# One tile of adj held for tests in layer 1, and table switches kept out from a logarithm's table load to its use

## The chip, the cores and the metric

One core of one Trainium2 chip. The metric is the device time of one execution in microseconds. The core has five engines with a queue each: TensorE (PE in the profile, its weight loads PEld), VectorE (DVE), ScalarE (ACT), GpSimd (POOL) and SyncE (SP), which here only issues transfers. Each queue runs in the order in which the program was written out; engines wait for each other through semaphores.

## The reference

Four graph layers over the same 4096 x 4096 matrix adj of zeros and ones (0.8% ones) and features x of 4096 x 64. Each layer adds its result to x after a layer norm and a relu.

```python
h = relu(layernorm(x)); x = x + L0(h, adj)   # weights 2^-(place among the last 100 neighbours), by a running count
h = relu(layernorm(x)); x = x + L1(h, adj)   # att = adj * sigmoid(scores(q, k)); support = att @ h; scaled
h = relu(layernorm(x)); x = x + L2(h, adj)   # twice: m = adj @ (x @ W); GRU gates with sigmoid and tanh
h = relu(layernorm(x)); x = x + L3(h, adj)   # hyperbolic: norms, artanh (logarithms), tanh, adj @ (gamma * X)
```

Layer 3's lines that matter here:

```python
_artanh(x) = arctanh(clip(x, -ARTANH_BOUND, ARTANH_BOUND))
mobius_matvec: res = tanh(mx_norm / x_norm * artanh(x_norm)) * (mx / mx_norm)
```

## The kernel before

The kernel keeps all of adj, transposed, in on-chip memory as 8-bit numbers (tiles A). Its 4096 columns are cut into four quarters q of 1024, worked on one after another; within a quarter the 4096 rows are 32 blocks of 128. The fast path is valid only where adj holds nothing but zeros and ones, so a second reading of adj in full precision is tested beside the other work: tiles named whole, 128 x 1024, 512 KB each, one DVE instruction and an accumulator read per tile. The count of other values goes through a small PE matmul (flag_ps) into a flag, which selects a general path at the end. There are 128 such tests in all. The generator checks() (lines 1102 to 1126) issues each transfer on SP's queue and then the test on DVE; the variable depth says how many further tiles it may have loaded beyond the test that is next. It was set to 2 in layer 0 (lines 1218 and 1221) and stays so in layer 1; in layer 2 it is 4.

Layer 1 (stream1, line 1347) takes a quarter in sixteen double blocks, two at a time. For each double block and each half c of the columns, score() makes two PSUM banks of scores on PE, weigh() (line 1328) takes the sigmoid of both on ACT into one tile sig and multiplies it with adj on DVE, and add() multiplies it with S on PE into the quarter's accumulators acc. So a pair of double blocks is 16 short score matmul records, 16 acc records, four sig tiles. The tiles sig and the tiles whole come from one pool, b4p (line 812), with six buffers:

```python
    b4p = ctx.enter_context(tc.tile_pool(name="fb4", bufs=6))
                loaded.append(b4p.tile([P, 2 * CW], F32, tag="b4", name="whole"))
        g = b4p.tile([P, 2, CW], F32, tag="b4", name="sig")
```

A new tile gets a buffer that an earlier one leaves, and its first writer (a transfer or a sigmoid) waits for the earlier tile's last reader. When a quarter ends, its accumulators are copied (mt) and added (agg), and post1 runs a long row of small steps beside the next quarter: the transpose ps_n, norms, a layer norm, the split into bf16 parts (hm, rest, lo) and the transpose ps_t.

The order of all this is written out beforehand by a planner, the class Weave. It books a guessed time for each instruction. The main loops issue their instructions directly; side work (generators such as post1, pre3, post3, checks) hands out one operation (Op) at a time, and draw() and fill() place it where begin(op) plus its guessed length fits before a limit. For DVE and ACT that limit is PE's planned time plus 0.4 plus weave.late, which is 1.0 in layer 1 once layer 0's side work is over (line 1375). Nothing of the planner runs on the chip; it fixes the order only.

Layer 3 prepares its features in pre3 (line 1638), once for each quarter, beside layer 2's second step and layer 3's first sums: two squares (of h and of mxn), their sums, lengths() (an inverse square root of twelve small DVE steps), artanh2() with two logarithms on ACT, a tanh, then three bf16 parts written to S3. ACT needs another table for the logarithm than for sigmoid or tanh. preload() runs a dummy activation (void) so that the table load stands early. Meanwhile the gates of layer 2's last quarter also use ACT: sigmoids r and z, and a tanh on r; then three DVE steps on xT and the transpose ps_o. Layer 3's sums (sum3) fill PSUM banks acc3, two for each of eight output blocks u; a new bank waits until its former reader is through. post3 does the last norm, artanh and tanh, and stores.

Of the kernel before, what the change touches and what calls it, by code (L numbers as in the profile page):

```python
# [12 lines left out]
AF = mybir.ActivationFunctionType  # L13
# [580 lines left out]
class Op:  # L594


    def __init__(self, e, dur, ins, outs, run, kinds=()):
        self.e, self.dur, self.ins, self.outs, self.run, self.kinds = e, dur, ins, outs, run, kinds


def names(*aps):
    return [a.tensor.name for a in aps if isinstance(a, bass.AP)]


class Weave:
# [10 lines left out]
    def __init__(self):  # L616
        self.t = dict.fromkeys("PDAGS", 0.0)
        self.at, self.used = {}, {}
        self.banks = {1: [0.0] * 8}
        self.kind = {}  # L620
        self.work, self.back, self.width = [], [], 2
        self.late = 0.0
        self.quiet = False
        self.dma = 0.0
        self.busy = False
        self.table = None
        self.tiled = 0

    def ready(self, e, ins, outs=(), kinds=()):
        s = 0.0  # L630
# [46 lines left out]
            (self.work if piece in self.work else self.back).remove(piece)  # L677

    def begin(self, op):
        return max(self.t[op.e], self.ready(op.e, op.ins, op.outs, op.kinds))  # L680

    def issue(self, piece):
# [62 lines left out]
TABLES = {AF.Sigmoid: 0, AF.Tanh: 0, AF.Ln: 1, AF.Exp: 2}  # L745


class Engine:
# [12 lines left out]
    def __getattr__(self, name):  # L761
        fn, w = getattr(self.real, name), self.weave

        def call(*args, **kw):
            outs = names(args[0], kw.get("accum_out"))
            ins = names(*args[1:], *(v for k, v in kw.items() if k != "accum_out"))
            n = max(math.prod(a.shape[1:]) for a in args if isinstance(a, bass.AP))
            dur = self.cost(name, n) if name != "dma_start" else 0.1
            if "accum_out" in kw:
                dur += 0.08  # L770

            def run():
                more = 0.0
                if name == "activation" and args[2] in TABLES:
                    more = 1.3 if w.table != TABLES[args[2]] else 0.0
                    w.table = TABLES[args[2]]
                w.book(self.e, dur + more, ins, outs)
                if name == "dma_start":
                    for k in outs:
                        w.land(k, 1.4 if "whole" in k else 0.8)  # L780
                return fn(*args, **kw)  # L781

            if self.later:
                return Op(self.e, dur, ins, outs, run)
            if self.e in "DA":
                w.fill(self.e, w.ready(self.e, ins, outs) + w.late)
            return run()
        return call
# [3 lines left out]
def fast_kernel(ctx: ExitStack, tc: tile.TileContext, t: dict, out: bass.AP, flag: bass.AP):  # L792
# [24 lines left out]
    weave = Weave()  # L817
# [282 lines left out]
    depth = [1]  # L1100
# [246 lines left out]
    def stream1():  # L1347

        acc, behind = [], []

        def add(c, q, i, gs):
            if i == 0:
                acc.append(one(f"acc{c}"))
            for j in range(2):
                b = 2 * i + j
                mm(acc[c][j * D:(j + 1) * D, :], S1[b // QB][:, b % QB, :], gs[c][:, j, :],
                   start=i == 0, stop=i == NB // 2 - 1)

        def add_behind(more=()):
            q, i, gs = behind.pop(0)  # L1360
            for c in (0, 1):
                add(c, q, i, gs)
                if more:
                    more.pop(0)()
                weave.draw(weave.quiet)
            if i == NB // 2 - 1:
                weave.finish()
                weave.add(post1(q, acc[:]))
                acc.clear()

        def turn(q, i, later=None):
            if q == 0 and i % (QB // 2) == 0:
                weave.until((1, i // (QB // 2)), DONE)
            weave.quiet = (1, NQ - 1) not in DONE
            weave.late = 2.0 if weave.quiet else 1.0
            gs = ahead[:] if (q, i) == (0, 0) else []
            for c in range(len(gs), 2):
                ps = score(q, i, c)
                if later is None:
                    gs.append(weigh(q, i, c, ps))  # L1380
                else:
                    later.append(lambda q=q, i=i, c=c, ps=ps: gs.append(weigh(q, i, c, ps)))
                weave.draw(weave.quiet or c == 1)
            behind.append((q, i, gs))
            if i == 8:
                load1(q + 1)

        for q in range(NQ):
            for i in range(0, NB // 2, 2):

                later = []
                turn(q, i)
                turn(q, i + 1, later)
                while len(behind) > 2:
                    add_behind(later)
                for go in later:
                    go()
                if len(behind) > 1:
                    add_behind()
        add_behind()  # L1400
# [193 lines left out]
        yield from pre3(q)  # L1594


    def lengths(s):

        yield DV.tensor_scalar(s, s, NORM_EPS2, None, op0=ALU.max)
        r = yield from rsqrt(s)  # L1600
        n = stat("norm", s.shape[1])
        yield DV.tensor_tensor(n, s, r, ALU.mult)
        return n, r
# [5 lines left out]
    def preload(func):  # L1609

        yield AC.activation(void, tab, func)

    def artanh2(x, between=()):

        nb = x.shape[1]
        xc = stat("axc", nb)
        yield DV.tensor_scalar(xc, x, ARTANH_BOUND, None, op0=ALU.min)
        q, r = stat("at", nb), stat("ln", nb)
        yield AC.activation(q, xc, AF.Ln, bias=ones)
        yield AC.activation(r, xc, AF.Ln, bias=ones, scale=-1.0)  # L1620
        yield from preload(AF.Tanh)
        low = small.tile([P, ST], I32, tag="st", name="flow")[:, :nb]
        yield DV.tensor_scalar(low, xc, 0.25, None, op0=ALU.is_lt)
        x2, p = stat("x2", nb), stat("po", nb)
        yield DV.tensor_tensor(x2, xc, xc, ALU.mult)
        yield DV.tensor_scalar(p, x2, *(2.0 * c for c in ARTANH_POLY[:2]), op0=ALU.mult, op1=ALU.add)
        yield DV.tensor_tensor(p, p, x2, ALU.mult)
        for c in ARTANH_POLY[2:-1]:
            yield DV.scalar_tensor_tensor(p, p, 2.0 * c, x2, op0=ALU.add, op1=ALU.mult)
        yield DV.tensor_tensor(q, q, r, ALU.subtract)  # L1630
        yield DV.scalar_tensor_tensor(p, p, 2.0 * ARTANH_POLY[-1], xc, op0=ALU.add, op1=ALU.mult)
        yield from between
        yield DV.copy_predicated(q, low, p)
        return q
# [3 lines left out]
    def pre3(q):  # L1638
# [8 lines left out]
        ss = stat("ss", 2 * QB)  # L1647
        for i, v in enumerate((hn, mx)):
            sq = b2("sq")
            yield AC.activation(sq, v, AF.Square)  # L1650
            yield DV.tensor_reduce(ss[:, i * QB:(i + 1) * QB], sq, AX.X, ALU.add)
        yield from preload(AF.Ln)
        n, r = yield from lengths(ss)
        mr, c = r[:, QB:], stat("ratio", QB)
        yield DV.tensor_tensor(c, n[:, QB:], r[:, :QB], ALU.mult)
        a = yield from artanh2(n[:, :QB])
# [10 lines left out]
        e = D + 1  # L1667
# [133 lines left out]
    def post3(parts3, sgn, den, ss):  # L1801

        nb = CB * len(parts3)
        part = [slice(i * CB, (i + 1) * CB) for i in range(len(parts3))]
        vs = [n65[:, :, :D] for u, (n65, al) in parts3]
        yield from head3(len(parts3) - 1, parts3[-1][1], sgn, den, ss)  # L1810
        yield from preload(AF.Ln)
        rd = yield from recip(den)
        n, r = yield from lengths(ss)
        t = stat("t", nb)
        yield DV.tensor_tensor(t, n[:, :nb], rd, ALU.mult)
        ratio = stat("ratio", nb)

        def between():
            yield DV.tensor_tensor(ratio, n[:, nb:], r[:, :nb], ALU.mult)

        a = yield from artanh2(t, between())
        for h, (u, (n65, al)) in zip(part, parts3):
            yield DV.scalar_tensor_tensor(a[:, h], a[:, h], 0.25, al, op0=ALU.mult, op1=ALU.mult)
        yield DV.scalar_tensor_tensor(a, a, ARTANH_MAX, ratio, op0=ALU.min, op1=ALU.mult)
        yield AC.activation(a, a, AF.Tanh)
        yield DV.tensor_tensor(a, a, r[:, nb:], ALU.mult)
        for h, v, (u, (n65, al)) in zip(part, vs, parts3):
            yield DV.scalar_tensor_tensor(v, v, 0.0, rows(a[:, h]), op0=ALU.max, op1=ALU.mult)
            x = X[u // 2][:, (u % 2) * CB:(u % 2 + 1) * CB, :]
            yield DV.tensor_tensor(x, x, v, ALU.add)  # L1830
            yield SY.dma_start(out_nm[:, u * CB:(u + 1) * CB, :], x)
# [8 lines left out]
    weave.add(pre0(NQ - 2))  # L1840
    stream0()
    lead[0] = math.inf
    stream1()
    depth[0] = 4
    for step in range(2):
# [89 lines left out]
```

## Time and profile before

| | us |
|---|---|
| median of 3 runs | 806.51 (806.50 to 806.54) |
| the profiled execution | 807.01 |
| its span in the profile | 805.1 |
| mean granted TensorE clock | 0.993 |

| stage | from, to in the span (us) |
|---|---|
| layer 0 (and the start of layer 1's side work) | 0 to about 240 |
| layer 1 | about 240 to 497 |
| layer 2, two steps | 497 to about 691 |
| layer 3's sums | in between, from about 691 to 790.6 |
| the last rows | 790.6 to 805.1 |

How to read it: a row of the timeline or the chain starts with the time from the span's start and a length. A group row names line, engine, operation, output<-input with shapes, and count; most DVE and ACT rows have line 781 and the PE rows 973, since helpers record them, so tiles are told apart by name. "[1.35 <-DVE whole]" means that the engine had been idle for 1.35 us and that this instruction of DVE, which writes or reads whole, released it. A run "x16" of PE is merged from 16 records, and its length can hold short pauses between them.

### The profile page before, as it was taken

The page shows a single profiled execution, that of the slowest core. Times are in us where ns is not written, and L with a number is a line of the kernel's source. Part 1 is how long each engine was busy: PE and PEld are TensorE (multiplying, and loading weights), DVE is VectorE, ACT ScalarE, POOL GpSimd, SP SyncE. Part 2 cuts the span into 40 slices and gives each one's busy share as a digit, 9 for nine tenths or more (in the row PEclk, how much of TensorE's full clock was granted, in tenths as well). Part 3 has the DMA queues.
Part 4 walks back from the last instruction along what each step waited for, and adds up shares of the span by engine and source line. Part 5 has one row for each costly group of instructions (what it writes and reads, how often), then busy time and mean ns, then how long its engine had stood idle before and what let it go on. Part 6 is the DMA issues. An engine that isn't in the chain of part 4 may idle for free.

```text
span 805.1 us, 12309 instructions
## 1 busy us (share of the span) xinstructions
PE 767.5 (95%) x4473; PEld 369.7 (46%) x4494; DVE 635.6 (79%) x1419; ACT 432.2 (54%) x756; POOL 61.6 (8%) x125
## 2 busy tenths in 40 slices
PE   5999999999999999998999999999999999999992
PEld 2334444544443333332333333444444444599992
DVE  6886867777777988988888898978789387685895
ACT  5655555565566777887787785113220245444333
POOL 3333233231000000000000000000000000000000
PEclk9999999999999999999999999999999999999997
DMA  9999999999601033013104006696888300000010
GB/s 220 153 174 193 217 163 207 205 177 207 183 34 40 0 118 93 25 59 99 52 25 130 30 1 210 225 361 215 287 304 313 76 8 20 1 2 2 9 35 17
DMA packets 43956, 98.41 MB, mean 122 GB/s; under 512 B 5104, under 2 KB 20464, under 8 KB 43888
## 3 DMA queue, kind: packets, MB, share of 16 engines
q1 hardware_dynamic: 25888, 78.98, 29.0%
q0 software_dynamic: 15840, 14.42, 19.1%
q10 hardware_dynamic: 2160, 4.14, 1.4%
q8 instruction: 37, 0.61, 0.3%
q14 instruction: 31, 0.25, 0.1%
HBM read 135.54 MB, written 5.24 MB: 175 GB/s over the span
## 4 chain that ended last, share of the span: by engine, by line
PE 80%; DVE 9%; ACT 6%; issue 2%; DMA 1%; SPq 0%; ACTq 0%; DVEq 0%
PE acc L973 50%; PE cnt L973 13%; PE score L973 10%; ACT sig L781 5%; DVE sig L781 3%; DVE whole L781 2%; PE rz L973 2%; PE ps_l L973 2%; DMA whole<-in_adjT 1%; PE ps_t L977 1%; PE ih L973 1%; ACT w L781 1%; DVE ss L781 1%; PE ps_kq L973 1%; DVE w L781 1%
## 5 line engine op out<-in xcount | busy, mean ns | idle before, releaser
L781 ACT ACTIVATE sig<-score,fatt_add,fatt_mul 128x512 f32<-128x512 f32 x256 | 179.2, 779 | 57.1 <-DVE whole L781 25.2
L781 DVE TENSOR_TENSOR sig<-sig,A 128x1024 f32<-128x1024 f32 x128 | 154.9, 1223 | 29.9 <-ACT sig L781 25.5
L781 ACT ACTIVATE w<-cnt 128x512 int16<-128x512 f32 x198 | 111.6, 595 | 88.6 <-PE cnt L973 85.7
L781 DVE SCALAR_TENSOR_TENSOR whole<-whole 128x1024 f32<-128x1024 f32 x128 | 153.2, 1220 | 4.6 <-DMA whole<-in_adjT 4.0
L973 PE MATMUL score<-qd,kT 64*128 64x512 f32 x512 | 126.3, 612 | 1.5 <-ACT sig L781 1.5
L973 PE MATMUL acc<-sig,S 128*64 128x512 f32 x512 | 120.2, 601 | 4.2 <-DVE sig L781 3.9
L973 PE MATMUL acc<-A,hm 128*128 128x512 fp8e4 x512 | 115.4, 379 | 0.0
L973 PEld LDWEIGHTS <-hm 128*128 128x128 bf16 x768 | 73.6, 98 | 90.3 <-issue 8.2
L973 PE MATMUL cnt<-A,ftri 128*128 128x512 fp8e4 x256 | 98.2, 386 | 8.2 <-ACT A L781 8.2
L973 PE MATMUL cnt<-A,fupd 128*128 128x512 fp8e4 x248 | 95.4, 385 | 4.0 <-ACT w L781 1.7
L973 PE MATMUL acc<-S,A 128*128 128x196 bf16 x1024 | 88.0, 246 | 0.0
L973 PEld LDWEIGHTS <-A 128*128 128x128 fp8e4 x1024 | 87.0, 96 | 1.3 <-issue 1.2
L973 PEld LDWEIGHTS score<-qd,kT 64*128 64x128 f32 x512 | 50.5, 186 | 72.0 <-issue 46.7
L973 PE MATMUL acc<-w,hm 128*128 128x512 bf16 x235 | 70.6, 379 | 0.9 <-issue 0.2
L781 DVE TENSOR_SCALAR w<-cnt 128x512 int16<-128x512 f32 x58 | 40.1, 691 | 39.5 <-PE cnt L973 38.3
L973 PEld LDWEIGHTS acc<-sig,S 128*64 128x64 f32 x512 | 32.5, 136 | 83.5 <-issue 40.8
L857 POOL DMA_DIRECT2D A<-in_adjT x110 | 59.9, 546 | 131.5 <-DMA A<-in_adjT 130.7
L973 PEld LDWEIGHTS <-lo 128*64 128x64 bf16 x768 | 39.8, 109 | 50.3 <-issue 21.3
L973 PE MATMUL acc<-A,lo 128*64 128x512 fp8e4 x512 | 58.9, 380 | 0.0
L781 ACT ACTIVATE mt<-acc 64x512 f32<-64x512 f32 x32 | 19.0, 592 | 74.2 <-PE acc L973 64.5
L973 PEld LDWEIGHTS <-ftri 128*128 128x128 bf16 x256 | 24.8, 98 | 47.4 <-issue 20.5
L1676 POOL MEMSET S<- 128x4 bf16 x8 | 0.9, 115 | 537.3 <-DVE xT L781 463.8
(185 smaller groups left out, 634.7 us busy)
## 6 DMA issues: line engine op xcount, KB each, us to landing
whole<-in_adjT SPq DMA_DIRECT2D x128, 512.0 KB, 6.7
A<-in_adjT POOLq DMA_DIRECT2D x110, 128.0 KB, 14.0
qd<-qs SPq DMA_DIRECT2D x16, 128.0 KB, 4.4
mx<-gs SPq DMA_DIRECT2D x16, 128.0 KB, 7.6
xT<-gs SPq DMA_DIRECT2D x8, 256.0 KB, 6.9
x<-in_x SPq DMA_DIRECT2D x6, 256.0 KB, 6.1
xs<-x SPq DMA_DIRECT2D x4, 256.0 KB, 6.0
qs<-qT ACTq DMA_DIRECT2D x4, 256.0 KB, 4.9
```

The lines of the kernel that those rows point to most:

```text
L781: return fn(*args, **kw)
L857: nc.gpsimd.dma_start(A8[q][b // 2][:, b % 2, :], a)
L973: nc.tensor.matmul(o, lhsT, rhs, start=start, stop=stop, skip_group_check=True)
L977: nc.tensor.transpose(o, src, ident)
L1676: nc.gpsimd.memset(S3[q, c][:, :, 3 * e:], 1.0)
```

## The change

Three edits. In layer 1, checks() may hold one tile beyond the next test instead of two (depth), and the planner's slack for side work there is 0.8 instead of 1.0. In layer 3, the logarithm's preload moves into lengths(), behind its first DVE step, and from there until both logarithms are issued the planner refuses to place any side operation of ACT which needs another function's table (held). Operations that need no particular table (copies, squares) and those that the main loops issue directly aren't held.

```diff
@@ class Op @@
-    def __init__(self, e, dur, ins, outs, run, kinds=()):
+    def __init__(self, e, dur, ins, outs, run, kinds=(), table=None):
         self.e, self.dur, self.ins, self.outs, self.run, self.kinds = e, dur, ins, outs, run, kinds
+        self.table = table
@@ class Weave @@
+        self.held = 0
     def begin(self, op):
+        if self.held and op.table not in (None, TABLES[AF.Ln]):
+            return math.inf
         return max(self.t[op.e], self.ready(op.e, op.ins, op.outs, op.kinds))
@@ class Engine @@
-                return Op(self.e, dur, ins, outs, run)
+                return Op(self.e, dur, ins, outs, run,
+                          table=TABLES.get(args[2]) if name == "activation" else None)
@@ stream1, turn @@
-            weave.late = 2.0 if weave.quiet else 1.0
+            weave.late = 2.0 if weave.quiet else 0.8
@@ lengths @@
-    def lengths(s):
+    def lengths(s, log=False):
         yield DV.tensor_scalar(s, s, NORM_EPS2, None, op0=ALU.max)
+        if log:
+            yield from preload(AF.Ln)
+            weave.held += 1
         r = yield from rsqrt(s)
@@ artanh2 @@
         yield AC.activation(r, xc, AF.Ln, bias=ones, scale=-1.0)
+        weave.held -= 1
         yield from preload(AF.Tanh)
@@ pre3 @@
-        yield from preload(AF.Ln)
-        n, r = yield from lengths(ss)
+        n, r = yield from lengths(ss, True)
@@ post3 @@
-        yield from preload(AF.Ln)
         rd = yield from recip(den)
-        n, r = yield from lengths(ss)
+        n, r = yield from lengths(ss, True)
@@ fast_kernel @@
     lead[0] = math.inf
+    depth[0] = 1
     stream1()
     depth[0] = 4
```

## The prediction

> **What bounds the kernel now.** I read the page first, then busy time by stage, then the waits of layer 1 alone, then the timeline of one quarter change, and last the stretch of layer 3 in which the second edit acts. The page's shares say TensorE (PE), but not where it waits:
>
> ```profile
> PE 767.5 (95%) x4473; PEld 369.7 (46%) x4494; DVE 635.6 (79%) x1419; ACT 432.2 (54%) x756; POOL 61.6 (8%) x125
> PE 80%; DVE 9%; ACT 6%; issue 2%; DMA 1%; SPq 0%; ACTq 0%; DVEq 0%
> ```
>
> The chain runs over PE for 80% of the span. The other 20% is what a change of waits can earn. The stages, cut at the points where layer 1's quarters of columns change:
>
> ```profile
> 253.90:317.77 63.87, 61.83 (x272) 22.94 (x270) 53.40 (x86) 46.75 (x72) 0.00 (x0) 1.00 0.20 66
> 317.77:381.31 63.54, 61.30 (x266) 21.81 (x268) 55.26 (x76) 48.91 (x72) 0.00 (x0) 1.00 0.22 67
> 381.31:444.85 63.54, 61.30 (x266) 21.81 (x268) 55.25 (x76) 48.91 (x72) 0.00 (x0) 1.00 0.22 67
> ```
>
> Columns are the window, its length, then busy time of PE, PEld, DVE, ACT and POOL. A quarter is eight pairs of blocks. A pair costs 3.72 us of score matmuls and 3.58 us of acc matmuls (undisturbed rows of the chain), so 8 x 7.30 = 58.4, and the two transposes ps_n and ps_t of 0.66 make 59.7. The quarter takes 63.54: 3.8 us are lost, of which 2.24 show as idle PE and the rest hides inside matmul runs that are longer than they should be. The waits of ScalarE (ACT) and PE from 285 to 497 us (total, times, longest):
>
> ```profile
> ACT sig L781 <- DVE whole L781: 25.2, 18, 2.3
> PE acc L973 <- DVE sig L781: 3.0, 7, 0.6
> PE ps_n L977 <- ACT sig L781: 2.3, 3, 0.8
> PE score L973 <- ACT sig L781: 1.5, 3, 0.5
> ```
>
> ACT's sigmoid stands 18 times, 25.2 us in all, for a test of adj on VectorE (DVE). No data flows from test to sigmoid. Both draw tiles from the six buffers of one pool (b4), and the sigmoid's tile lies where the tested tile lay. One change of quarter shows what that costs PE:
>
> ```profile
> 378.49 1.23 DVE L781 SCALAR_TENSOR_TENSOR whole<-whole 128x1024 f32<-128x1024 f32 x1
> 379.82 1.45 ACT L781 ACTIVATE sig<-score,fatt_add,fatt_mul 128x512 f32<-128x512 f32 x2 [1.35 <-DVE whole L781]
> 380.65 0.66 PE L977 MATMUL ps_n<-fident,agg 128*128 128x128 f32 x4 [0.81 <-ACT sig L781]
> 382.44 1.22 DVE L781 SCALAR_TENSOR_TENSOR whole<-whole 128x1024 f32<-128x1024 f32 x1
> 448.37 4.67 PE L973 MATMUL score<-qd,kT 64*128 64x512 f32 x16
> 456.55 3.79 PE L973 MATMUL score<-qd,kT 64*128 64x512 f32 x16
> ```
>
> The sigmoid waits 1.35 for the test, so a PSUM bank comes free late, so the transpose ps_n waits 0.81. The last two rows are equal runs of 16 score matmuls: the one behind a change of quarter takes 0.88 longer, with no idle mark.
>
> **What the Trainium skill says.** "Perfetto Trace Analysis", section "Optimization Strategy", says that the same gap repeating on the engine that should be saturated can mean that there are too few buffers for the next tile; the trace agrees, with the 18 waits above. The same page, "Identifying the Most-Contended Engine", warns that matmul busy time is no measure of headroom; so the 61.30 of 63.54 above is read against the sum of undisturbed runs. "ScalarE: Activation LUTs", "What ACT_TABLE_LOAD costs", gives about 1283 ns for a load plus a drain of about 1380; here a load takes 1.28 us, and z starts at 710.86 behind a load of 1.28 from 709.57, so no drain is added and 1.28 is used. "DMA: Bandwidth & Descriptors", "Anatomy of one DMA", says that semaphore waits happen on the issuing sequencer and not in the DMA engines: a transfer whose buffer isn't free holds every later one of SP's queue. The trace fits: one row of SP holds five issues of whole spread over 18.88 us.
>
> **Part 1, depth 1 and the planner's slack of 0.8 in layer 1.** Costs come from the rows above and the order of instructions in the changed program as built.
>
> Removed: one of two tile buffers held by tests. With two tiles ahead, four or five of layer 1's sigmoids get a buffer whose test stands directly beside their own multiplication in DVE's queue. In the changed order 15 sigmoids still follow a test in their buffer, but from the second on at least two multiplications of other tiles (2 x 1.22 us) stand between, so the test is done when the scores are. The tests between first and last multiplication fall from 21 to 19, and the pairs of neighbouring tests at blocks 13 and 14 of the second and third quarter become single ones. Post1's later pieces move one block pair later because of 0.8. What PE regains:
> - ps_n's waits, 0.69 + 0.81 + 0.81 = 2.3. The sigmoid ahead of it no longer waits for the test. All of it goes: 2.3 (at least 1.5).
> - The lengthened score run, 3 x 0.88 = 2.6. Its cause is the next sigmoid, which stood 1.76 for the second test of the change (idle before ACT's row at 383.71); it now follows the first test, done two multiplications before. I take 2.6 (at least 1.3, if the square of ps_n ahead of it on ACT sets the start).
> - acc waiting for multiplied tiles, 3.0. Of this 0.26 + 0.26 at 494 to 496 us is the end of the stage and stays. Of the other 2.5 I take 2.0, since at 292.25 a test waits 1.02 us for its transfer in both programs (between 0.9 and 2.5).
> - Scores waiting for a sigmoid behind the two mt copies, 1.5. The copies (2 x 0.59) stay; a sigmoid ahead of them is no longer held by the newest acc, so half: 0.7 (0 to 1.5).
> Sum 7.6.
>
> Added: a transfer starts only after the test before it. It takes 3.9 us (median, issue to landing, in this stretch; least 3.7). The shortest distance is the second test at a change of quarter. Its transfer waits in SP's queue for the buffer that the first acc of the new quarter releases, about 374.6 in the second change (371.79 plus three quarters of 3.58, and the issue); landed at 378.8, needed at 382.4. Slack 3.6 us, cost 0. Behind it in SP's queue stand the reload of X (256 KB, 4.9 us) and the next tile; both are needed over 5 us later.
>
> Moved: two tests to layer 2, 64 there become 66, 2 x 1.22 = 2.4 us on DVE. PE has no gap between 497 and 680 (busy 63.00 of 63.00 and 60.00 of 60.00 in two windows), DVE is at 83 to 86%. PE's matmuls cover the tests: 0. If that cover fails, mx or the flag matmul is late; the flag stands 16 matmuls of 0.11 and 16 of 0.22, 5 us, later in the changed order, more than 2.4, so at most 2 us are at risk, through mx.
>
> **Part 2, tables kept out.** The table loads keep their number. In the last block of layer 3's preparation the order on ACT and DVE turns:
>
> ```profile
> 703.07 0.69 ACT L781 ACTIVATE r<-rz,gate_b 128x512 f32<-128x512 f32 x1
> 709.57 1.28 ACT L781 ACT_TABLE_LOAD   x1
> 710.86 0.69 ACT L781 ACTIVATE z<-rz,gate_b 128x512 f32<-128x512 f32 x1
> 711.68 0.17 DVE L781 TENSOR_TENSOR gam<-at 128x8 f32<-128x8 f32 x1 [1.82 <-ACT at L781]
> 718.93 0.63 PE L977 MATMUL ps_o<-fident,xT 128*128 128x128 f32 x4 [1.63 <-DVE xT L781]
> ```
>
> The load and z leave the space between logarithm and tanh, so gam comes about 3.4 us earlier. PE stands only at ps_o, 1.63, and z moving behind would lengthen that; but ps_o itself stands four matmuls later, and xT, worked through row by row (S pieces done at 711.2, n and alpha to 711.6, load to 712.9, z to 713.5, tanh to 714.2, three steps on xT between three pairs of n), is ready at about 718. PE gets there at about 719.3. The 1.63 goes. In exchange the first step on r (r<-ih) now stands behind the clamp of at, and its PSUM bank is the one that the third early sum's second half needs. PE is there at 701.56 + 1.01 + 48 x 0.086 = 706.7. The square of mxn moves ahead of the load, so sums and root start at 703.2 instead of 705.2; the clamp ends 4.1 later (4.69 in the trace less 0.6 of the interposed r), at 707.5, r<-ih at 708.2: PE waits 1.5. Net -0.1, taken as 0; bounds: a loss of 1.5 (both waits stand), a gain of 1.6 (none does). S3 of the third quarter is 3 us earlier, needed only at about 736 (the S3_2 sums follow 176 matmuls of 86 ns, and two short groups, behind ps_o), so worth nothing. The tail from 790.6 on keeps its chain.
>
> **Sum.** Span 805.1, execution 807.0; less 7.6 gives 799.4. The median of the runs shown is 0.5 below that execution: 799.0 (798.9 rounded).
>
> **Rivals.** About 0.2% (1.6 us) is the least that can be told from no change here.
> - The wait changes its name: sigmoids freed of tests wait for acc or for scores (10.4 and 11.4 us in the same window already), and PE keeps the mt waits and half of the rest. For it: ACT is busy 48.9 of 63.5. Against: it had idled those 25.2 us. Gain 3.5: 803.
> - Layer 3's new bank wait and a late mx in layer 2 take back 3: 802. For it: DVE is one queue, and small chains slip. Against: layer 2 shows no gap at all.
> - Slower: one tile ahead no longer hides its transfer. Place: second test at each change of quarter, and one more per quarter. If SP starts that transfer only where the trace has the next one (382.36), it lands at 386.3 and DVE stands 3.9, all multiplications behind it too. A block's second tile has a slack of 1.45 (score 0.93, two tiles of sigmoids 2.90, multiplication 1.22, against its acc 6.51 after the pair's start), so PE loses 2.5; six times is 15 against the 7.6: 814. It decides once six transfers land about 6.3 us later than worked out (3.6 + 1.45 + 7.6 / 6). Against: their buffers are free before.
> - The buffers are dealt as before in effect, the waits stay: 806.5.
>
> **How the numbers follow.** Forecast 0.66, first rival 0.14, second 0.08, slower 0.08, none 0.04. So faster 0.88, same 0.04, slower 0.08. The forecast's own bounds (5.2 to 8.9 in layer 1 with partial failures, -1.5 to +1.6 in layer 3, -2 to 0 in layer 2) give 797 to 802; with the first two rivals in, 797.0 to 803.5 holds about eight in ten.
>
> **What would show it.** Right: ACT sig waiting for DVE whole falls from 25.2 to under 5 us, ps_n's wait on ACT sig is gone, quarters last about 61 us instead of 63.5, score runs stay at 3.8, the wait at ps_o is gone and one of about 1.5 stands at an acc of layer 3 near 700. Wrong: DVE whole waits for DMA more than 1.0 in layer 1, PE gaps in layer 2, or a chain that still holds DVE whole in layer 1.

## The result, and the profile after

| | before | after |
|---|---|---|
| median (us) | 806.50 (806.33 to 806.54, 4 runs) | 797.16 (796.93 to 797.33, 4 runs) |
| span of the profiled execution | 805.1 | 794.9 |
| end of layer 1 (first acc of layer 2) | 496.70 | 486.47 |
| end of layer 3's sums | 790.63 | 780.67 |

The time falls by 9.3 us; the ratio is 0.9884, with a 95% interval of 0.9867 to 0.9901. The two profiled executions (807.01 and 796.93) lie 10.1 apart, and layer 1 gives all of that (both kernels are at the same matmul within 0.17 us at 255, and 10.23 apart at 496.70 and 486.47). From there to the end of the sums both kernels need the same: 293.93 before, 294.20 after.

The helper lines now are 785 (DVE and ACT) and 978 and 982 (PE). The page of the kernel after: busy time of the engines, shares of the chain that ended last, and the group of sigmoids.

```profile
PE 764.1 (96%) x4473; PEld 369.8 (47%) x4494; DVE 636.8 (80%) x1419; ACT 429.7 (54%) x756; POOL 61.5 (8%) x125
...
PE 87%; DVE 6%; ACT 3%; DMA 1%; issue 1%; SPq 0%; ACTq 0%; DVEq 0%
...
L785 ACT ACTIVATE sig<-score,fatt_add,fatt_mul 128x512 f32<-128x512 f32 x256 | 177.3, 784 | 47.7 <-PE score L978 40.8
```

The chain runs over PE for 87% instead of 80%. ACT's sigmoids still idle for 47.7 us, but 40.8 of that is now a wait for scores, so for PE, the engine that bounds the stage. Busy time by quarter of layer 1 (window, length, then PE, PEld, DVE, ACT, POOL, clock, share and GB/s of the transfers):

```profile
253.90:315.31 61.41, 61.08 (x267) 23.10 (x264) 52.71 (x85) 46.02 (x72) 0.00 (x0) 1.00 0.18 61
315.31:375.47 60.16, 60.16 (x266) 22.04 (x266) 54.38 (x74) 48.14 (x73) 0.00 (x0) 1.00 0.20 62
375.47:435.63 60.16, 60.16 (x266) 22.05 (x266) 54.38 (x74) 48.14 (x72) 0.00 (x0) 1.00 0.20 62
```

A full quarter takes 60.16 instead of 63.54, and PE is busy through all of it. The undisturbed runs added up to 59.7, so 0.5 is left. The waits of ACT from 285 to 490 us (total, times, longest); the same question for PE has no line at all:

```profile
ACT sig L785 <- PE score L978: 34.2, 25, 1.9
...
ACT sig L785 <- DVE whole L785: 1.9, 2, 1.1
```

One change of quarter, from the timelines of ACT, DVE and PE:

```profile
372.57 2.79 ACT L785 ACTIVATE sig<-score,fatt_add,fatt_mul 128x512 f32<-128x512 f32 x4 [0.60 <-PE score L978]
...
373.47 1.23 DVE L785 SCALAR_TENSOR_TENSOR whole<-whole 128x1024 f32<-128x1024 f32 x1
...
375.40 0.66 PE L982 MATMUL ps_n<-fident,agg 128*128 128x128 f32 x4
...
376.89 1.22 DVE L785 SCALAR_TENSOR_TENSOR whole<-whole 128x1024 f32<-128x1024 f32 x1
...
379.57 3.84 PE L978 MATMUL score<-qd,kT 64*128 64x512 f32 x16
```

Both tests are still there, 3.4 us apart, but no sigmoid waits for either, ps_n starts without a wait, and the score run behind the change takes 3.84 instead of 4.67. One loss stays: as before the change, the stage's first fetched tile comes late for its test, and the acc run beside it takes 4.28 where undisturbed ones take 3.65:

```profile
292.09 1.23 DVE L785 SCALAR_TENSOR_TENSOR whole<-whole 128x1024 f32<-128x1024 f32 x1 [1.03 <-DMA whole<-in_adjT]
...
292.45 4.28 PE L978 MATMUL acc<-sig,S 128*64 128x512 f32 x16
```

In layer 3's preparation the timelines of DVE and PE read:

```profile
697.66 0.74 DVE L785 SCALAR_TENSOR_TENSOR r<-ih,W,r 128x512 f32<-128x512 f32 x1
...
698.46 11.04 PE L978 MATMUL acc<-S,A 128*128 128x196 bf16 x128 [1.17 <-DVE r L785]
709.34 0.60 PE L982 MATMUL ps_o<-fident,xT 128*128 128x128 f32 x4
```

The wait of 1.63 at ps_o is gone; one of 1.17 stands at an acc whose bank waits for r.

A word on depth, which the section on the change counts one too high: checks() loads until it has depth tiles and takes the tile of its next test from them. So with depth 1 it holds that tile alone, and the next fetch is written right behind the test; with depth 2 it holds one more. Where this document speaks of one or two tiles ahead, it counts from the test written last.

### The profile page after: what moved, and what is told of

It reads as the page before. It is cut to its first block, busy times and chain, and to the rows that moved or that the text cites. A ratio compares the mean times of both kernels' runs of the same rounds, so it can differ in the third digit from the quotient of the medians.

```text
span 794.9 us, 12299 instructions
## 1 busy us (share of the span) xinstructions
PE 764.1 (96%) x4473; PEld 369.8 (47%) x4494; DVE 636.8 (80%) x1419; ACT 429.7 (54%) x756; POOL 61.5 (8%) x125
## 3 DMA queue, kind: packets, MB, share of 16 engines
q10 hardware_dynamic: 2160, 4.14, 1.4%
## 4 chain that ended last, share of the span: by engine, by line
PE 87%; DVE 6%; ACT 3%; DMA 1%; issue 1%; SPq 0%; ACTq 0%; DVEq 0%
PE acc L978 54%; PE score L978 13%; PE cnt L978 13%; PE rz L978 2%; PE ps_l L978 2%; DMA whole<-in_adjT 1%; ACT sig L785 1%; PE ps_t L982 1%; DVE sig L785 1%; DVE ss L785 1%; PE ih L978 1%; ACT w L785 1%; DVE nt L785 1%; PE ps_kq L978 1%; DVE w L785 1%
## 5 line engine op out<-in xcount | busy, mean ns | idle before, releaser
L785 ACT ACTIVATE sig<-score,fatt_add,fatt_mul 128x512 f32<-128x512 f32 x256 | 177.3, 784 | 47.7 <-PE score L978 40.8
L978 PE MATMUL score<-qd,kT 64*128 64x512 f32 x512 | 124.4, 609 | 0.0
L862 POOL DMA_DIRECT2D A<-in_adjT x110 | 59.7, 544 | 132.3 <-DMA A<-in_adjT 131.5
```

The costliest lines, as they stand in the source:

```text
L862: nc.gpsimd.dma_start(A8[q][b // 2][:, b % 2, :], a)
L978: nc.tensor.matmul(o, lhsT, rhs, start=start, stop=stop, skip_group_check=True)
```

## The experiments

The first four take the change apart. Each was timed against the kernel before.

**Depth alone.**

```diff
@@ fast_kernel of the kernel before @@
+    depth[0] = 1
     stream1()
```

> The kernel before with depth 1 in layer 1 alone (slack 1.0 and the table code stay). Theory A (what costs time is the sigmoid that gets a buffer whose test stands beside its own multiplication; depth decides this): nearly all of layer 1's gain is here, ACT sig waiting for DVE whole under 4 us, quarters of about 60.3, 797 to 799 us. The wait at ps_o in layer 3 (1.63) stays, since ACT's order is that of before. Theory B (the slack of 0.8 spaces the tests on DVE and carries the gain): 802 to 805 us, quarters of 62 or more.

Measured: 797.12 us (796.39 to 798.04), ratio 0.9886, interval 0.9871 to 0.9901. ACT's and DVE's waits from 285 to 490 us, then busy time in a quarter, then the row of ps_o in PE's timeline:

```profile
ACT sig L781 <- DVE whole L781: 1.8, 2, 1.2
...
DVE whole L781 <- DMA whole<-in_adjT: 5.6, 4, 1.8
```

```profile
315.00:375.13 60.13, 60.13 (x265) 22.05 (x264) 54.08 (x74) 48.15 (x73) 0.00 (x0) 1.00 0.20 62
```

```profile
708.53 0.63 PE L977 MATMUL ps_o<-fident,xT 128*128 128x128 f32 x4 [1.62 <-DVE xT L781]
```

This is the gain of the whole change from one line (layer 1 ends at 486.00), as theory A had it. The wait at ps_o stays. DVE's tests wait four times for their transfer here, up to 1.8 us, which the kernel after does once (1.03); PE still has no marked wait in that window, so such waits were hidden.

**The slack alone.**

```diff
@@ stream1, turn @@
-            weave.late = 2.0 if weave.quiet else 1.0
+            weave.late = 2.0 if weave.quiet else 0.8
```

> The kernel before with the slack 0.8 in layer 1 alone (depth 2 stays). Theory A: five sigmoids still stand next to a test with no other multiplication between, and thirteen with one; a part of the waits stays, quarters of 62.3 to 63.5, 802 to 806 us. Theory B: 798 to 801 us. Both: if this edit turned ACT's order in layer 3's preparation, the wait of 1.63 at ps_o is gone here and one of about 1.2 stands at an acc.

Measured: 803.79 us (803.68 to 804.17), ratio 0.9965, interval 0.9952 to 0.9979. ACT's largest wait and PE's wait at ps_n from 285 to 490 us, then layer 3 in PE's timeline:

```profile
ACT sig L781 <- DVE whole L781: 16.0, 16, 2.1
...
PE ps_n L977 <- ACT sig L781: 0.7, 1, 0.7
```

```profile
705.34 11.04 PE L973 MATMUL acc<-S,A 128*128 128x196 bf16 x128 [1.17 <-DVE r L781]
```

The slack moves tests by a place and so frees some sigmoids: layer 1 ends 3.0 us earlier. It does not add to depth's gain, which has those waits already. And it is this edit that turns the order in layer 3: here, without any table code, ps_o's wait is gone and the acc waits 1.17, and ACT's order in that stretch is the one of the kernel after.

**A seventh buffer, the order untouched.**

```diff
@@ pools of the kernel before @@
-    b1p = ctx.enter_context(tc.tile_pool(name="fb1", bufs=8))
-    b2p = ctx.enter_context(tc.tile_pool(name="fb2", bufs=20))
-    b4p = ctx.enter_context(tc.tile_pool(name="fb4", bufs=6))
-    small = ctx.enter_context(tc.tile_pool(name="fsmall", bufs=22))
+    b1p = ctx.enter_context(tc.tile_pool(name="fb1", bufs=7))
+    b2p = ctx.enter_context(tc.tile_pool(name="fb2", bufs=19))
+    b4p = ctx.enter_context(tc.tile_pool(name="fb4", bufs=7))
+    small = ctx.enter_context(tc.tile_pool(name="fsmall", bufs=20))
```

> The kernel before with seven buffers in the pool of sig and whole instead of six (room for it from the pools of small tiles); the order on every engine is that of before, tests, depth 2 and slack 1.0 too. Theory A: the same order with one more buffer loses most of the waits, 797.5 to 800 us, ACT sig waiting for DVE whole under 5 us. Theory C (the tests' time on DVE, 1.22 each, pushes the multiplications, and the buffer is only where it shows): the order on DVE is unchanged, so 805 to 807 us, and the sigmoids' waits take another name.

Measured: 796.47 us (796.39 to 796.62), ratio 0.9874, interval 0.9859 to 0.9889. One quarter by engine:

```profile
315.90:376.06 60.16, 60.16 (x266) 22.02 (x265) 55.26 (x76) 48.32 (x73) 0.00 (x0) 1.00 0.23 71
```

DVE is busy for the same 55.26 as before the change, with the same tests in the same places, and yet the quarter takes 60.16. So it isn't the tests' time on DVE that cost PE; it is that a sigmoid had to write where a tested tile lay. Theory C falls, and the time is even under theory A's.

The buffer may be worth more than the median says. Taking the stage from the transpose ps_t at 255 us to the first acc of layer 2, layer 1 lasts 241.66 before, 231.60 after, 231.30 with depth alone, and 229.46 here (257.28 to 486.74). But layer 1 begins 2.2 us later. Beside the seventh buffer only the smaller pools differ, and in layer 0 a cnt matmul now waits 1.01 for a w, which it did not before:

```profile
231.22 0.38 PE L973 MATMUL cnt<-A,fupd 128*128 128x512 fp8e4 x1 [1.01 <-DVE w L781]
...
257.28 0.66 PE L977 MATMUL ps_t<-fident,h 128*128 128x128 f32 x4
```

How much of the shorter stage is the buffer's and how much is only the late start made good (1.2 us of it fall between 257 and 286) was not tried.

**The table code alone.**

```diff
@@ lengths, artanh2, Weave.begin: all of the edit on tables, nothing else @@
+        if log:
+            yield from preload(AF.Ln)
+            weave.held += 1
...
+        weave.held -= 1
```

> The kernel before with the table part alone. As built, the order on all engines is that of before: 806.5 us, within 0.1%, in every theory; ACT sig waiting for DVE whole stays at about 25 us and the wait of 1.63 at ps_o stays. If it is faster by more than 0.2%, the table code acts in a way that the order doesn't show.

Measured: 806.62 us, ratio 1.0, interval 0.9992 to 1.0009. ACT's waits from 285 to 490 us, and ps_o in PE's timeline:

```profile
ACT sig L785 <- DVE whole L785: 21.8, 16, 2.3
```

```profile
718.89 0.63 PE L982 MATMUL ps_o<-fident,xT 128*128 128x128 f32 x4 [1.62 <-DVE xT L785]
```

The order is that of before on all engines, and so is the time. (In the same window sigmoids wait 24.1 for tests before; the profile puts one wait of 2.3 down to an acc here, and both names together give 34.5 in either run.) The gates' z, which stood between logarithm and tanh, is placed when both logarithms have been issued, and there the hold is already over.

**What layer 1 gains if it has no tests at all.**

```diff
@@ Weave.pieces, and around stream1 in the kernel after @@
-        return self.work[:self.width] + ([] if self.quiet else self.back)
+        return self.work[:self.width] + ([] if self.quiet or self.still else self.back)
...
+    weave.still = True
     stream1()
+    weave.still = False
```

> The kernel after, with no test of adj in layer 1 at all: all 19 of its tests go to layer 2, 85 there instead of 66. Layer 1 can win what is left: the wait of about 1.0 of the first test for its transfer and little more, 0.4 to 1.5 us. Theory F (PE's matmuls in layer 2 cover any test, as the prediction put it for two): 795.7 to 797 us. Theory G (layer 2's DVE is nearly full; 17 to 19 tests of 1.22 more, 23 us, don't fit beside it): 800 to 812 us, with PE waiting for mx or the tests running on into layer 3's sums.

Measured: 817.9 us, ratio 1.0138, interval 1.0121 to 1.0155. Layer 1 ends at 487.08, no earlier than with 19 tests (486.47), so the tests' time on DVE no longer bounds it. (A tile that had been fetched keeps its buffer meanwhile, so that the stage isn't quite free of them.) Later, from the timelines of DVE and PE:

```profile
754.71 1.23 DVE L786 SCALAR_TENSOR_TENSOR whole<-whole 128x1024 f32<-128x1024 f32 x1
...
699.84 15.06 PE L979 MATMUL acc<-S,A 128*128 128x196 bf16 x156 [4.14 <-ACT r L786]
...
757.02 11.59 PE L979 MATMUL acc<-S,A 128*128 128x196 bf16 x108 [4.63 <-DVE n L786]
```

The last 16 tests don't fit into layer 2. They stand in layer 3, almost without a break from 735.34 to 755.94, and the sums wait 4.63 for the n behind them. Theory G. The sums end at 792.3, 11.6 later than in the kernel after: 8.8 are the two waits, and the clock sinks behind each (last section). The rows behind the sums take 23.8 instead of 14.2, since DVE has their steps still to do.

**The remaining wait in layer 3.** The only difference from depth alone is that the planner is told that the last xT is ready 2 us later.

```diff
@@ post2b @@
         DONE.add(("gates", q))
+        if q == NQ - 1:
+            for k in names(o):
+                weave.at[k] = weave.at[k][0] + 2.0, "D"
```

> Depth 1 alone, and the transpose ps_o of layer 2's last quarter moved 48 matmuls (48 x 0.086 = 4.1 us) back in PE's order; with it ps_t and ps_l move 32 matmuls back. Nothing else turns. Theory D (the wait of 1.62 at ps_o lies on the path that sets the end, whichever edit leaves it there): the wait goes, 797.1 - 1.6 = 795.5 us. Rival E (what ps_o feeds, the last quarter's features of layer 3, becomes late in its place): a new wait of PE behind ps_l or at the last sums, 796.5 to 798 us.

Measured: 796.08 us (795.62 to 796.35), ratio 0.9866, interval 0.9849 to 0.9882. In the trace ps_o has no wait, and this is the only wait of PE from 500 us to the end of the sums:

```profile
716.98 0.63 PE L977 MATMUL ps_t<-fident,h 128*128 128x128 f32 x4 [0.23 <-DVE h L781]
```

So 1.62 - 0.23 = 1.4 should be won; the medians show 1.0 against depth alone. Nearly theory D, with a trace of E.

> As the run with ps_o moved, and seven buffers instead of six in the pool of sig and whole. Theory A (buffers): at depth 1 the sixth buffer already frees the sigmoids from the tests, so the seventh adds under 0.5 us: 795.0 to 795.6 us. If the two gains add up (10 of seven buffers on top of 10 of depth), layer 1 would have to run faster than its matmuls, which I don't expect: 786 us.

With seven buffers as well (the pools as above): 795.51 us (795.40 to 795.74), ratio 0.9861, interval 0.9844 to 0.9877. The two ways out of the same wait don't add up (layer 1 ends at 486.58), and layer 0 pays for the smaller pools here too. This version is 1.65 us, 0.2%, under the kernel after, just at the edge of what can be told apart.

**How near is depth 1 to a late transfer?** This asks for the price of the slower rival. In the kernel after, each tile of layer 1 is fetched twice.

```diff
@@ checks, kernel after @@
                 Y_.dma_start(loaded[-1], adjT[b * P:(b + 1) * P, c * 2 * CW:(c + 1) * 2 * CW])
+                if depth[0] == 1:
+                    nc.sync.dma_start(loaded[-1], adjT[b * P:(b + 1) * P, c * 2 * CW:(c + 1) * 2 * CW])
```

> The kernel after, with each tile for a test of layer 1 fetched twice in a row into the same buffer, so that it lands about 3.9 us later; the order on PE, ACT and DVE stays. The prediction's slower rival rests on such a delay: it gave the second test of a quarter's change a slack of 3.6 us. If that slack holds: DVE waits of 0.3 to 1 at three tests, hidden mostly, 797 to 799 us. If the real slack is near 1.8 (the trace of after issues that transfer at about 311.0 and tests at 316.7, less 3.9): waits of about 2 at each change, of which the scores' slack hides a part, 798 to 803 us. If depth 1 stands on the edge: 806 us or more.

Measured: 809.61 us (808.28 to 811.28), ratio 1.0035, interval 1.002 to 1.0049. The two fetches (SP) and the two tests (DVE) of one change of quarter:

```profile
379.17 0.33 SPq L785 DMA_DIRECT2D whole<-in_adjT  x1
383.01 0.33 SPq L1118 DMA_DIRECT2D whole<-in_adjT  x1
...
381.98 1.22 DVE L785 SCALAR_TENSOR_TENSOR whole<-whole 128x1024 f32<-128x1024 f32 x1
...
387.18 1.23 DVE L785 SCALAR_TENSOR_TENSOR whole<-whole 128x1024 f32<-128x1024 f32 x1 [1.69 <-DMA whole<-in_adjT]
```

DVE wanted the second test at 387.18 - 1.69 = 385.49. The first fetch had landed at about 379.17 + 3.9 = 383.1. So a single transfer has 2.4 us to spare here; the second fetch overdraws that. Four waits of DVE (4.91, 3.21, 1.69, 1.83) end layer 1 at 497.06, 10.6 later. (By the order of the changed program, the second fetch also changes how the buffers are dealt; what that costs, no trace here shows.) The last three stand at changes of quarter and go with 2.5, 1.0 and 1.1 us. The first goes with most, 6.0 us up to the next ps_n (321.26 instead of 315.24), and it is no change of quarter: it is the stage's first fetched tile, which was 1.03 late already, and PE stands still behind it:

```profile
295.97 1.23 DVE L785 SCALAR_TENSOR_TENSOR whole<-whole 128x1024 f32<-128x1024 f32 x1 [4.91 <-DMA whole<-in_adjT]
...
298.40 3.68 PE L978 MATMUL acc<-sig,S 128*64 128x512 f32 x8 [4.01 <-DVE sig L785]
```

All the gain of the change goes with one more transfer time for each tile.

Was it the landing, or SP's queue, which stands while the second fetch waits for the first? Three runs were to tell.

> Seven buffers, depth 2 and slack 1.0 (the kernel that took 796.5), with each tile for a test of layer 1 fetched twice in a row into the same buffer, as was done to the kernel after (which then took 809.6, 12.4 more). Theory H (with one tile ahead the later landing reaches DVE, and two tiles ahead would have hidden it): DVE waits little for transfers, 796.5 to 800 us. Theory I (not the landing, but SP's queue, blocked by the second fetch for 3.9 us each time, delays the other loads of layer 1): the same blocking is here, so 804 to 810 us.

> The kernel after (depth 1), each tile for a test of layer 1 fetched twice as before, but the second fetch from GpSimd's queue, which is empty in layer 1; so the tile lands late again while SP's queue isn't held. Theory H (the later landing reaches DVE: slack 2.2 to 2.4 at a change of quarter against some 4 us more): DVE still waits for DMA by 1.5 to 2 at each change and more at the first test, 801 to 810 us. Theory I (the run with both fetches on SP, 809.6, was slow because SP's queue stood): little is left of the loss, 797 to 800 us.

> Seven buffers and depth 2, the second fetch from GpSimd's queue. With SP free, two tiles can be under way at once. Theory H: the second tile ahead hides the later landing, 796.5 to 799 us, DVE waiting for DMA by little more than 1 in layer 1; the 822.0 with both fetches on SP then came from SP's queue. If it is over 805 us, two tiles ahead don't hide 8 us of transfer either, and the order of the tests (three in a short row at each change) is what needs the early landing.

The first run has this edit for depth 2 in the kernel with seven buffers. The other two issue the second fetch from GpSimd's queue, in the kernel after and with seven buffers:

```diff
-                    nc.sync.dma_start(loaded[-1], adjT[b * P:(b + 1) * P, c * 2 * CW:(c + 1) * 2 * CW])
+                    nc.gpsimd.dma_start(loaded[-1], adjT[b * P:(b + 1) * P, c * 2 * CW:(c + 1) * 2 * CW])
```

Measured: 821.98 us (ratio 1.0191, interval 1.0174 to 1.0208), 821.16 (1.0183, 1.0166 to 1.02) and 829.12 (1.028, 1.0263 to 1.0297). A test of DVE in the second run, at the same change of quarter as above:

```profile
389.67 1.23 DVE L785 SCALAR_TENSOR_TENSOR whole<-whole 128x1024 f32<-128x1024 f32 x1 [2.90 <-DMA whole<-in_adjT]
```

In the first run, the second test at that change, and a load of layer 2 that stood behind second fetches on SP's queue:

```profile
386.94 1.22 DVE L781 SCALAR_TENSOR_TENSOR whole<-whole 128x1024 f32<-128x1024 f32 x1
...
514.82 1.01 PE L973 MATMUL ps_g<-m 128*128 128x192 f32 x2 [5.72 <-DMA m<-in_consts]
```

And three tests in a row in the third run:

```profile
360.73 1.22 DVE L781 SCALAR_TENSOR_TENSOR whole<-whole 128x1024 f32<-128x1024 f32 x1
...
364.40 1.22 DVE L781 SCALAR_TENSOR_TENSOR whole<-whole 128x1024 f32<-128x1024 f32 x1
...
371.96 1.22 DVE L781 SCALAR_TENSOR_TENSOR whole<-whole 128x1024 f32<-128x1024 f32 x1 [6.33 <-DMA whole<-in_adjT]
```

Freeing SP's queue didn't help, so theory I falls as the main cause: the late landing reaches DVE. The runs don't price the standing queue, though. From GpSimd's queue the pair of fetches takes longer (9.2 us from the first issue at 380.46 to the test, 8.0 with both on SP), and in the first run the queue does cost something: PE stands 5.72 for m. By the times, the other half of theory H falls too; in the traces it holds where it was meant. At the changes of quarter no second test waits with depth 2, in either run, where depth 1 has 1.7 to 3.2. The loss is elsewhere. With depth 2 the planner sets three tests close together (the third was wanted at 371.96 - 6.33 = 365.63, 4.9 after the first), and the third tile is fetched only once the first is handed out for its test; a doubled transfer comes too late for that, whichever queue issues it. What two tiles ahead are worth against a small delay stays open. In the profiled execution of the third run layer 1 ends 20.7 us later than with seven buffers alone (507.44 and 486.74); behind it PE waits 3.9 and 2.1 for g and agg.

**Depth 1 where no sigmoid shares the buffers.**

```diff
@@ fast_kernel of the kernel after @@
     stream1()
-    depth[0] = 4
```

> The kernel after, with depth left at 1 in layer 2 and on instead of 4; no sigmoid shares the buffers there. If one tile ahead is as good as four wherever the transfer fits between two tests: 797 to 798 us. In layer 2 a test follows the last one by less than 3 us in the trace of after (66 in about 130 us), and a transfer takes 3.9 us and more, so DVE should stand for DMA at most of them, the tests run on beyond layer 2 and PE waits: 810 to 860 us. There is then no gain of depth 1 by itself; it pays only where it frees a buffer that another engine waits for.

Measured: 848.18 us (846.88 to 848.75), ratio 1.051, interval 1.0493 to 1.0528. Layer 1 is that of after (its end is 486.52). The planner knows of the transfers, so DVE hardly waits for them; it spaces the tests out, and 33 are left for layer 3, where they stand in a row from 732.24 to 775.04 and one acc waits behind them:

```profile
776.12 35.51 PE L978 MATMUL acc<-S,A 128*128 128x196 bf16 x384 [27.59 <-DVE n L785]
```

In that row a test follows the last in 1.1 to 2.0 us and DVE waits at most 0.8 for a transfer, at depth 1, though one transfer takes some 3.9: SP's queue runs ahead of DVE where buffers are free. So depth is a rule for the order that the planner writes, and the loss here comes from where the planner put the tests. Fewer tiles ahead is no gain in itself.

## Why the prediction was right, and where it wasn't

The forecast of 799.0 came out 1.8 us high; 797.16 is only 0.2 above the low end of its range. Its mechanism for layer 1, buffers in common, is what the runs show; its cause for layer 3 is not. By its steps, with times taken from the start of one run of matmuls to the start of the next, so that pauses inside runs count:

- **ps_n, 2.3.** All three waits (0.69, 0.81, 0.81) are gone. Right. (This was the gap that repeats on PE, the engine that should be saturated; the 18 waits that the prediction names beside that sign stand on ACT.)
- **The lengthened score run, 3 x 0.88 = 2.6.** All three runs now take 3.84 for 4.67: 3 x 0.83 = 2.5. Right.
- **acc waiting for multiplied tiles, 2.0 of 3.0.** The marks all went, and 4.1 us with them: the four runs take 0.52, 1.37, 1.38 and 0.87 less, since a broken run costs more than its marks (see the last section). At 292 I was right to keep a part: 0.6 stays there, behind the test that still waits for its transfer. What I had kept as "the end of the stage" was not: those two waits were sigmoids held up further ahead, and with them gone the stage ends in one run of 24 without a mark. Under by 2.1.
- **Scores behind the mt copies, 0.7 of 1.5.** The marks of 1.5 went, and the runs up to ps_n take 3.87, 3.99 and 3.99 in place of 4.47: 1.6 us. Undisturbed they take 3.71, so 0.7 stays without a mark, near the 0.8 that I had kept for the copies; whether it is theirs was not tried. Under by 0.9.
- **Not in the sum: a loss of 0.4.** Score runs elsewhere take 3.84 in place of 3.79.
- The sum for layer 1 was 7.6 and should have been 2.3 + 2.5 + 4.1 + 1.6 - 0.4 = 10.1, as measured. Only 6.6 of that show as less idle time of PE; 3.6 lay inside its runs (from 253.9 us to the end of the stage its records sum to 235.75 before and 232.14 after, for the same matmuls). I had priced those terms by their marks and then discounted terms of one cause one by one, as if each could stay while the others went. The seventh buffer and depth alone show that nearly all go together.
- **Transfers at cost 0.** Right, but the slack of 3.6 was too generous. The trace of after has the issue at 370.7, a landing some 3.9 later and the test at 376.89: 2.3. The doubled fetch gives 2.4. And the change of quarter is not the shortest distance: at 292 a tile is 1.03 late, before the change as after it. My sign of being wrong, DVE waiting more than 1.0, was set too low: with 1.8 in depth alone, layer 1 is no longer than in the kernel after.
- **Two tests moved to layer 2 at cost 0.** Without its marked waits, the way from the end of layer 1 to the end of the sums takes 292.3 with 64 tests there (before, and seven buffers) and 292.6 to 293.0 in depth alone, slack alone and after, with 66. So 0.3 to 0.7. But two executions of the same instructions in layer 1 (depth alone, and with ps_o moved) differ by 0.9 at its end, so this is at the edge of what these traces tell.
- **Layer 3, net 0.** The trade came as written: 1.63 at ps_o went, a wait at the acc behind r came, 1.17 where I had 1.5. Net 0.46. Its cause was wrongly named: I put the turned order down to the edit on tables. It comes from the slack of 0.8, which shifts what the planner believes about all that follows; alone, the edit on tables moves no instruction. The number held because I had read the order of the changed program, which shows what turns and not which edit turns it; that part is luck, not understanding.
- **The rivals.** The wait did change its name: sigmoids now wait 34.2 us for scores, 11.4 before. That is no loss, since PE waits for nothing in return. For the slower rival I had worked out that six transfers must land 6.3 us late to eat the gain. That was too easy on the change: in the run with doubled fetches, four waits of DVE between 1.7 and 4.9 do it, and the changes of quarter, which I had named first, carry only 4.6 of the 10.6 us.

## What to carry to other kernels

A wait between two instructions that share no data can be a question of which tiles share buffers: ask who had the buffer last, and on which engine's queue that reader stands. One more buffer, or one tile less held by side work, was here worth nearly all the waits behind that one cause together, and a small shift of order only some of them. What is given up is time in which a transfer may be late, so look at every distance from the free buffer to the reader before holding fewer tiles (2.3 us at a change of quarter, none left at the stage's first fetched tile); where no other engine wants the buffers, as in layer 2, it only costs.

## What I had not expected

- A pause in a row of matmuls costs more than its mark. Before, 16 acc records that two waits (0.35 and 0.58) cut into three pieces read 1.94 + 1.08 + 1.08 = 4.10; in one piece they read 3.65. From their start at 363.11 to the next run at 368.07 are 4.96 us, in one piece 3.59: 1.37 lost where the marks say 0.93.

```profile
363.11 1.94 PE L973 MATMUL acc<-sig,S 128*64 128x512 f32 x8
365.40 1.08 PE L973 MATMUL acc<-sig,S 128*64 128x512 f32 x4 [0.35 <-DVE sig L781]
367.06 1.08 PE L973 MATMUL acc<-sig,S 128*64 128x512 f32 x4 [0.58 <-DVE sig L781]
```

- With a long wait of PE comes more: its granted clock sinks (the column ahead of the share of transfers). Two windows of the kernel without tests in layer 1, with the waits of 4.14 and 4.63 in them; then, for PE alone, one us ahead of the wait of 4.01 in the run with doubled fetches on SP, and one behind it:

```profile
690.00:740.00 50.00, 45.85 (x493) 42.83 (x492) 32.71 (x118) 20.62 (x50) 0.35 (x3) 0.97 0.05 14
740.00:792.00 52.00, 47.37 (x531) 46.62 (x530) 43.30 (x152) 12.28 (x45) 0.00 (x0) 0.93 0.27 98
...
293.00:294.00 1.00, 1.00 (x8) 1.00 0.96 184
...
299.00:300.00 1.00, 1.00 (x4) 0.50 0.81 291
```

At a clock of 0.50 PE gets through four acc records in the us in place of eight. Seen in slices of 10 us in all the traces shown here, from 20 us to the end of the sums, each of the 14 waits of PE of 2.8 us or more has a clock of 0.50 to 0.96 in its slice or the next, and none of the waits of up to 2.1 us has one; elsewhere the clock is 0.99 or 1.00. (In the first 20 us PE waits up to 6.1 us and the clock reads 1.00.) Traffic alone does not do it: the kernel after moves up to 352 GB/s in layer 2 at 1.00. That the wait itself is the cause was not tried.
